# Attention windows: transposes issued later, statistics spread out, depthwise taps moved to earlier stages

## The chip, the cores and the metric

The kernel runs on one core of a Trainium2 chip. Its engines are TensorE (matrix multiplications and transposes, PE in the profile; PEld is its weight load), VectorE (DVE), ScalarE (ACT), GpSimd (POOL) and SyncE (SP), which here only issues DMAs. Each engine works through its own queue in order. The metric is the device time of the whole program in microseconds, as the median of several executions. All times here are microseconds (us) unless marked otherwise.

## The reference

The program is a stack of four layers on `x`, a batch of 4 images with 256 channels of 64 x 64. Each layer is `x = x + layer(_gn(x))`. Layers 0 and 1 are attention layers of one form, with different weights; layers 2 and 3 are Mamba layers, whose code the change leaves alone. Cut to what matters:

```python
def mhsa(x, ...):                       # a gated scan along the height
    Z = tanh(conv1x1(tanh(conv1x1(x, w1a, b1a)), w2a, b2a))
    F = sigmoid(conv1x1(tanh(conv1x1(x, w1b, b1b)), w2b, b2b))
    # second half of the channels is flipped; then, from the last row to the first:
    h = f * h + (1.0 - f) * z

def ssa(x_img, ...):                    # attention of windows
    xw = to_windows(x_img)              # 8 x 8 windows of 8 x 8 pixels
    q, k, v = split(xw @ qkv_w.T + qkv_b)
    logit = einsum('bpc,bqc->bpq', q.mean(2) * SCALE, k.mean(2))
    _, idx = top_k(logit, 4)            # each window attends to 4 windows
    k_g, v_g = gather(k, idx), gather(v, idx)      # 4 * 64 keys
    attn = softmax(einsum('bphqd,bphkd->bphqk', qh * SCALE, kh))   # 8 heads of 32
    out = einsum('bphqk,bphkd->bphqd', attn, vh)
    out_img = from_windows(out) + depthwise_conv3x3(v_img, lepe_w) + lepe_b
    return out_img @ wo_w.T + wo_b

x = x + ssa(mhsa(_gn(x), ...), ...)     # layers 0 and 1
x = x + mamba(_gn(x), ...)              # layer 2
x = x + grouped_mamba(_gn(x), ...)      # layer 3
```

`_gn` normalises groups of two neighbouring image columns, each over all channels and rows: it subtracts the mean and divides by the root of the variance. A strip of the kernel, below, holds four such groups.

## The kernel before

One image is worked on at a time; `x` (256 channels in two halves of 128 partitions, 4096 pixels) stays on the chip through all four layers. The image is cut into 8 strips of 8 columns; a strip holds 8 windows.

**Order of work.** The attention layers run under a manual schedule: the order in which the program issues instructions is the order in which each engine executes them, and tiles are handed on by semaphores as soon as their last reader is done. A tile with `bufs=n` has n buffers; a new tile with the same tag waits until the buffer that it takes is free.

**Scan phase** (`scan_phase`). For each strip s it makes the four small convolutions of the gated scan, the scan on VectorE, and then `keys_values(s - 1)`: keys and values by `conv` (L232), values written into the padded image `vimg` (L357), copied on POOL into `vst` (L361), transposed on TensorE (L383), copied by VectorE and ScalarE into `vn` (L389, L390) and stored with the keys into DRAM. `lepe(lay, s, ...)` gives the steps of the 3 x 3 depthwise convolution of strip s in place in `vimg`, in two halves of the channels, m = 0 and 1: on VectorE nine steps for each m (L268 first, then L270), on POOL 17 for each m (L268 first, then eight pairs of a multiply L253, into a tile of tag "sq" with one buffer, and an add L256). Strips 0 to 4 are done in the scan phase on VectorE. The last call is `keys_values(7)`. Then `routing` finds the four windows for each window (L443 to L464), and the queries of strips 2 to 4 are made, with the m = 0 taps of strip 5 on VectorE between them and the m = 1 taps of strip 5 on POOL.

**Window phase** (`window_phase`). It runs over 32 pairs of windows, i = 0 to 31; `sj, a = divmod(i, 4)` gives the strip and the place in it. The eight heads are worked on in two parities h = 0 and 1. The names of the steps, with their lines:

- `gather(i)` issues eight DMAs on SP (L516) that fetch the keys and values of the pair; the buffers hold four pairs. `indices` loads the window numbers into SP's registers, `double(s)` copies queries (L308, L314).
- `scores(i, h)` on TensorE (L538) into one of two `sc` tiles; `smallest(i, h)` on VectorE (L550) gives the minimum, which is the maximum of the scores since the queries are negated; `exps(i, h, ...)` on ScalarE (L561) has four parts with their sums; `normalise(i, h)` takes the reciprocal on VectorE (L573) and multiplies on POOL in four parts (L576).
- `turn(i, h)` transposes the probabilities with eight instructions on TensorE (L589) into two tiles `pt_ps`, which have two buffers in all, so one turn fills both; `turned(h, 0)` copies the first to `pts` on VectorE (L600), `turned(h, 1)` the second on ScalarE (L602).
- `values(i)` multiplies with the values (L615), and `own_rows(i)` adds the result into `vimg` on VectorE (L626).
- `project(sj - 1, m)` makes the output convolution of a finished strip in the pairs with a = 1 and 2 (14 in all); its `add` (L636) adds into `x` at the pair's end. `query(...)` makes the late queries of strips 6 and 7 in pairs 19, 20, 23 and 24.

In pair i TensorE is given scores(i, 1), turn(i - 1, 1), the projection or query if there is one, scores(i + 1, 0), values(i - 1), turn(i, 0).

**Steps planned into the pairs.** `mids[i]` and `ends[i]` hold steps that run in pair i after the third and fourth exponential of parity 0, and at the pair's end. In the first layer they hold the normalisation of the first two strips for the next layer (`gn`): a sum on VectorE (L143), a column sum on TensorE (L134), the centring on POOL (L151), one square on ScalarE (L156, into a tile of tag "sq", which POOL's taps use too), a reduction (L160), a column sum and the scaling on POOL (L168, L172). In the second layer they hold `stats` of strips 0 to 6: a sum (L200), a column sum (L195), the mean (L206), four squares on ScalarE (L215), a column sum and the variance (L221). All column sums, projections and late queries share one PSUM bank (tag "mm"). What falls behind the last pair is returned in `left` and run by `attention_layers` with the projection of the last strip (`tail`). The taps of strip 6 and 7 are in the window phase: 51 steps on POOL, two per pair, and nine on VectorE in pairs 2 to 10 (`taps`, `dve_taps`).

Of the kernel before, what the change touches and what calls it, by code (L numbers as in the profile page):

```python
# [44 lines left out]
class Net:  # L45
# [33 lines left out]
    def attention_layers(self, x, w_drams, v_drams):  # L79
        tc, nc = self.tc, self.nc  # L80
        with ExitStack() as ctx:
# [107 lines left out]
            def stats(s, psum):  # L189
                xs = x.rearrange("p (c h w) -> p c w h", c=2, w=S)[:, :, strip[s], :]  # L190
                box = {}

                def columns(tag, part):
                    box[tag] = psum().tile([P, NT], F32, tag="mm", name=f"gn_{tag}")
                    nc.tensor.matmul(box[tag][:, 0:4], self.one_gn, part, start=True, stop=True)  # L195

                def sums():
                    box["s1"] = self.small.tile([P, 4], F32, tag="gn_s1", name="gn_s1")
                    xr = x.rearrange("p (n w) -> p n w", w=S)[:, :, strip[s]]
                    nc.vector.tensor_reduce(  # L200
                        box["s1"], xr.rearrange("p n (g t) -> p g n t", t=2), AX.XY, ALU.add
                    )
# [7 lines left out]
                def squares():  # L210
                    box["s2"] = self.small.tile([P, 4], F32, tag="gn_s2", name="gn_s2")
                    sq = norm.tile([P, 2, 8, S], F32, tag="xn", name="gn_sq")
                    for g in range(4):
                        two = slice(2 * g, 2 * g + 2)
                        nc.scalar.activation(  # L215
                            sq[:, :, two], xs[:, :, two], AF.Square,
                            bias=box["mean"][:, g : g + 1], accum_out=box["s2"][:, g : g + 1],
                        )
# [4 lines left out]
                return (  # L223
                    sums, lambda: columns("pm", box["s1"]), mean, squares,
                    lambda: columns("pv", box["s2"]), variance,
                )
# [90 lines left out]
            def scan_phase(lay, work, psum, tail):  # L317
# [78 lines left out]
                for s in range(NW):  # L396
# [32 lines left out]
                    if s in (5, 6):  # L429
                        for evict in [query(lay, s - 5, m, psum) for m in range(2)]:  # L430
                            evict()
                keys_values(NW - 1)

# [35 lines left out]
            def window_phase(lay, work, psum, idx, nxt):  # L469
# [183 lines left out]
                taps6, taps7 = (lepe(lay, s, pool=True) for s in (NW - 2, NW - 1))  # L653
                taps = taps6[17:] + taps7[17:] + taps7[:17]
                dve_taps = lepe(lay, NW - 2)[:9]
# [10 lines left out]
                if nxt:  # L666
                    load_scan_weights(nxt)
                    for s in range(2):
                        i = 10 + s
                        plan(gn(nxt, s, lambda: psum), (ends, i), (ends, i + 1), (mids, i + 2),  # L670
                             (ends, i + 2), (mids, i + 3), (ends, i + 5), (mids, i + 6))
                else:

                    for s in range(NW - 1):
                        i = 4 * s + 6
                        last = i + 6 if s < 5 else i + 3
                        plan(stats(s, lambda: psum), (ends, i), (ends, i + 1), (mids, i + 2),
                             (ends, i + 2), (ends, last), (mids, last + 1))
                for i in range(n_pair):
# [16 lines left out]
                    for t in taps[2 * i : 2 * i + 1]:  # L696
                        t()
# [6 lines left out]
                    exps(i, 1, (0, 1))  # L704
                    scores(i + 1, 0)
# [4 lines left out]
                    turn(i, 0)  # L710
# [21 lines left out]
                turned(0, 0)  # L732
                turned(0, 1)
                turn(n_pair - 1, 1)
                turned(1, 0)
                turned(1, 1)
# [20 lines left out]
            for i, lay in enumerate(layers):  # L757
                with tc.tile_pool(name=f"at_a{i}", bufs=1, reuse_waits="tile") as work, tc.tile_pool(
# [5 lines left out]
                    taps = lepe(lay, NW - 3, psum)[:9]  # L764
# [6 lines left out]
                    for t in lepe(lay, NW - 3, pool=True)[17:]:  # L771
                        t()
                with tc.tile_pool(name=f"at_c{i}", bufs=1, reuse_waits="tile") as work, tc.tile_pool(
# [3 lines left out]
                    box, tail, left = window_phase(lay, work, psum, idx, nxt)  # L777
# [1386 lines left out]
```

## Time and profile before

Three runs took 11993.68, 12002.51 and 12006.19 us, the median 12002.51.

| what | us |
|---|---|
| median of three runs | 12002.51 |
| profiled execution, its own time | 11985.03 |
| its span, first to last instruction | 11983.3 |
| PE busy in the span | 10083.2 (84%) |
| DVE busy | 9833.8 (82%) |
| POOL busy | 8811.5 (74%) |
| ACT busy | 7002.3 (58%) |
| mean granted TensorE clock | 0.932 |

The page lists groups of instructions by line, engine, operation and tiles, with their count, busy time and mean duration in ns, and what ended the engine's idle time before them. A wait reads "engine tile line <- who released it: total us, times, longest". A line of a timeline reads "start, duration, engine, line, operation, tiles, shapes, count [idle before it <- releaser]". The clock is the share of TensorE's full clock that it was granted.

The scan phase and routing of an attention layer take some 215 us, its window phase some 250 us; an image takes about 2995 us, of which the two attention layers are about 950. The window phases begin, by their first minimum reduction, at 233.3, 699.9, 3220.8, 3686.2, 6214.7, 6682.6, 9214.6 and 9678.1 us; first and second layer alternate.

### The profile page before, as it was taken

The numbers are of one execution on the slowest core, as the hardware profiler recorded it, in microseconds if no ns is written. First come the engines' busy times: TensorE is split into PE (matmuls) and PEld (weight loads), VectorE is DVE, ScalarE is ACT, GpSimd is POOL, SyncE is SP. The second block draws the span as 40 slices with busy tenths as digits, with TensorE's granted clock in tenths as the row PEclk, the third lists the DMA queues.
The fourth block names the chain that finished last, engine by engine and source line by source line (L and its number), as shares of the span: only waits on it lengthen the run. The fifth ranks groups of instructions, "written<-read, shape, count | busy, mean of one in ns | idle before, by whom it ended". The sixth has DMA issues, their size and how long they took to land.

```text
span 11983.3 us, 192241 instructions
## 1 busy us (share of the span) xinstructions
PE 10083.2 (84%) x71104; PEld 5778.2 (48%) x71104; DVE 9833.8 (82%) x8350; ACT 7002.3 (58%) x13096; POOL 8811.5 (74%) x6054
## 2 busy tenths in 40 slices
PE   8998887777899888777799988877778998887777
PEld 4564554444455455444445645544444554554444
DVE  6677998998666799899866779989986667998998
ACT  4555555776455555477645555547764555554776
POOL 4666886898456688689745668868984666887897
PEclk9999998999999899899999989989999999998999
DMA  3343454454334355445433434444543343454454
GB/s 96 100 126 134 174 175 149 169 180 160 92 98 127 134 173 177 145 169 182 159 90 99 128 132 173 174 148 167 180 160 91 100 127 135 173 176 146 169 176 154
DMA packets 682506, 1742.10 MB, mean 145 GB/s; under 512 B 88896, under 2 KB 194896, under 8 KB 681312
## 3 DMA queue, kind: packets, MB, share of 16 engines
q1 hardware_dynamic: 676448, 1721.41, 43.1%
q10 hardware_dynamic: 5120, 8.39, 0.3%
q8 instruction: 563, 9.22, 0.3%
q14 instruction: 375, 3.07, 0.1%
HBM read 1601.52 MB, written 94.39 MB: 142 GB/s over the span
## 4 chain that ended last, share of the span: by engine, by line
DVE 23%; PE 23%; ACT 8%; issue 5%; POOL 4%; DMA 1%; SPq 0%; DVEq 0%; POOLq 0%; ACTq 0%
DVE h L1002 13%; DVE pb L996 5%; PE conv_ps L232 4%; PE y L954 4%; PE u_ps L1291 3%; ACT da L938 2%; PE pb L926 1%; PE u_ps L1664 1%; POOL pr L576 1%; PE sc L538 1%; DVE lp L270 1%; PE pt_ps L589 1%; ACT dap L938 1%; PE z_ps L1316 1%; POOL hc L1008 1%
## 5 line engine op out<-in xcount | busy, mean ns | idle before, releaser
L1008 POOL TENSOR_TENSOR hc<-h,cb 128x1024 f32<-128x1024 f32 x2056 | 4809.6, 2350 | 806.4 <-DVE h L1002 350.9
L1002 DVE TENSOR_TENSOR_SCAN h<-da,m_state,pb 128x1024 f32<-128x1024 f32 x1248 | 2920.6, 2340 | 161.4 <-DVE pb L996 2.4
L954 PE MATMUL y<-ident,hc 128*128 128x128 f32 x16384 | 2333.6, 290 | 408.0 <-POOL hc L1008 340.9
L954 PEld LDWEIGHTS y<-ident,hc 128*128 128x128 f32 x16384 | 2034.5, 150 | 1124.9 <-POOL hc L1008 577.0
L996 DVE TENSOR_TENSOR pb<-du,pb 128x1024 f32<-128x1024 f32 x1672 | 2025.4, 1211 | 113.4 <-PE pb L926 110.9
L938 ACT ACTIVATE da<-delta,m_v 128x1024 f32<-128x1024 f32 x1672 | 1899.5, 1141 | 135.5 <-DVE h L1002 118.3
L926 PE MATMUL pb<-m_parts,pick 128*128 128x512 bf16 x3312 | 1078.2, 410 | 846.1 <-DVE h L1002 777.6
L576 POOL TENSOR_SCALAR pr<-pr,sm,zero 128x256 f32<-128x256 f32 x2048 | 1136.5, 569 | 476.8 <-DVE sm L573 475.8
L561 ACT ACTIVATE pr<-sc,mn 128x256 f32<-128x256 f32 x2048 | 955.9, 482 | 647.5 <-DVE sm L573 480.9
L926 PEld LDWEIGHTS <-pick 128*128 128x128 bf16 x3312 | 263.1, 101 | 1787.4 <-DVE h L1002 981.2
L550 DVE TENSOR_REDUCE mn<-sc 128x4 f32<-128x1024 f32 x512 | 627.9, 1228 | 550.0 <-PE sc L538 547.2
L1002 DVE TENSOR_TENSOR_SCAN h<-da,pb 128x1024 f32<-128x1024 f32 x424 | 969.5, 2287 | 55.1 <-DVE pb L996 0.9
L912 POOL TENSOR_TENSOR bb<-du,bb 128x1024 f32<-128x1024 f32 x376 | 888.6, 2363 | 88.8 <-DMA bb<-m_cd 84.0
L589 PE MATMUL pt_ps<-ident,pr 128*128 128x128 f32 x4096 | 705.4, 304 | 144.3 <-POOL pr L576 51.1
L1002 DVE TENSOR_TENSOR_SCAN h<-dap,m_state,bb 128x1024 f32<-128x1024 f32 x288 | 672.4, 2335 | 65.1 <-ACT dap L938 45.9
L232 PE MATMUL conv_ps<-att_y,att_wb 128*128 128x512 f32 x1536 | 683.3, 594 | 1.3 <-DVE gn_mean L206 1.3
L589 PEld LDWEIGHTS pt_ps<-ident,pr 128*128 128x128 f32 x4096 | 490.3, 151 | 307.5 <-POOL pr L576 161.7
L538 PE MATMUL sc<-kv,q_swap 32*64 32x128 f32 x8192 | 597.2, 287 | 6.7 <-DMA kv<-kv_dram 4.7
L938 ACT ACTIVATE dap<-delta,m_v 128x1024 f32<-128x1024 f32 x376 | 419.7, 1116 | 304.0 <-DVE h L1002 234.2
L538 PE MATMUL sc<-kv,att_y 32*64 32x128 f32 x7168 | 569.2, 287 | 11.8 <-DMA kv<-kv_dram 7.5
L538 PEld LDWEIGHTS sc<-kv,att_y 32*64 32x64 f32 x7168 | 430.0, 139 | 144.9 <-ACT pr L561 65.6
L270 DVE SCALAR_TENSOR_TENSOR lp<-vimg,att_v,lp 128x512 f32<-128x512 f32 x616 | 465.4, 756 | 28.1 <-DVE lp L270 1.4
(300 smaller groups left out, 17937.9 us busy)
## 6 DMA issues: line engine op xcount, KB each, us to landing
cb<-m_cd SPq DMA_DIRECT2D x2048, 512.0 KB, 3.8
kv<-kv_dram SPq DMA_DIRECT2D x1984, 128.0 KB, 2.8
bb<-m_cd SPq DMA_DIRECT2D x376, 512.0 KB, 5.4
kv_dram<-kst SPq DMA_DIRECT2D x128, 256.0 KB
kv_dram<-vn SPq DMA_DIRECT2D x128, 256.0 KB, 4.1
q_swap<-att_y SPq DMA_DIRECT2D x96, 256.0 KB, 4.3
m_pe<-in_pe_dram SPq DMA_DIRECT2D x32, 512.0 KB, 4.1
out_dram<-yo SPq DMA_DIRECT2D x64, 256.0 KB, 2.4
```

What stands on the lines that cost most here:

```text
L232: nc.tensor.matmul(ps, w[:, k, w0 + m * P : w0 + (m + 1) * P], src[:, k], start=(k == 0), stop=(k == 1),)
L538: nc.tensor.matmul(sc[h][b * 64 : b * 64 + 64, r, w, m, :], (own(sj, m) if r == b else swap[sj % 2][:, m])[rows, 2 * a + w], kv[i, w][rows ...
L561: nc.scalar.activation(t[:, g].rearrange("p j r t -> p r j t"), sc[h][:, :, g // 2, g % 2, :].rearrange("p r (j t) -> p r j t", j=2), AF.E ...
L576: nc.gpsimd.tensor_scalar(t[:, g], t[:, g], s[:, g : g + 1], self.zero, ALU.mult, ALU.add)
L589: nc.tensor.transpose(pt[h][j][:, g, :], t[:, g, j].rearrange("p r t -> p (r t)"), self.ident,)
L912: nc.gpsimd.tensor_tensor(pb[i], slots[i][0]["du"], pb[i], ALU.mult)
L926: nc.tensor.matmul(pb[i][:, ss], self.pick[:, n : n + 1].to_broadcast([P, P]), blk["parts"][:, ss], start=True, stop=True,)
L938: nc.scalar.activation(da[i], blk["delta"], AF.Exp, scale=blk["a"](n))
L954: nc.tensor.matmul(blk["y"][:, ss], t[:, ss], self.ident, is_transpose=True, start=(n == 0 and ss.start % NT == 0), stop=(n == DS - 1 and ...
L996: nc.vector.tensor_tensor(pb[i], blk["du"], pb[i], ALU.mult)
L1002: nc.vector.tensor_tensor_scan(h[i][:, ss], da[i][:, ss], pb[i][:, ss], state, ALU.mult, ALU.add)
L1008: nc.gpsimd.tensor_tensor(hc[i][:, ss], h[i][:, ss], cb[i][:, ss], ALU.mult)
```

## The change

- **Turns.** turn(i, 0) is no longer issued within pair i but at the start of pair i + 1, ahead of scores(i + 1, 1). turn(i - 1, 1) is issued in pair i ahead of scores(i + 1, 0), behind the steps of `mids` and the projection or query, where it was directly behind scores(i, 1). The evictions `turned` keep their places.
- **Squares, sums and norms.** In `stats` the four squares become four steps, each at a place of its own (end of one pair, middle and end of the next, middle of the third). The sum moves one pair later (a = 3, where there is no add); column sums follow in pairs with a = 0 and a = 3. In `gn` the two strips begin at pairs 7 and 11 and not at 10 and 11, and the square stands one pair behind the centring. The statistics of strip 6 fall behind the last pair.
- **Taps.** The m = 0 taps of strip 5 (nine, VectorE) and its m = 1 taps (17, POOL) go to the end of the scan phase: the nine and the first five of POOL ahead of keys_values(7), the other twelve behind it. The m = 0 taps of strip 6 take the place of those of strip 5 between the queries, nine of its POOL steps stand behind these, and the other eight go into the window phase. Strip 7 has its m = 1 taps on POOL in the window phase and its m = 0 taps on VectorE there. So POOL has 25 steps in the window phase, one per pair, and VectorE nine, in pairs with a = 0 or 3 from i = 3 to 19.

```diff
+                def square(g):
+                    if g == 0:
+                        box["s2"] = ...
+                        box["sq"] = norm.tile([P, 2, 8, S], F32, tag="xn", name="gn_sq")
+                    two = slice(2 * g, 2 * g + 2)
+                    nc.scalar.activation(
+                        box["sq"][:, :, two], xs[:, :, two], AF.Square,
+                        bias=box["mean"][:, g : g + 1], accum_out=box["s2"][:, g : g + 1],
+                    )
...
+                for t in lepe(lay, NW - 3, psum)[:9]:
+                    t()
+                later = lepe(lay, NW - 3, pool=True)[17:]
+                for t in later[:5]:
+                    t()
                 keys_values(NW - 1)
+                for t in later[5:]:
+                    t()
...
-                taps6, taps7 = (lepe(lay, s, pool=True) for s in (NW - 2, NW - 1))
-                taps = taps6[17:] + taps7[17:] + taps7[:17]
-                dve_taps = lepe(lay, NW - 2)[:9]
+                taps = taps + lepe(lay, NW - 1, pool=True)[17:]
+                dve_taps = lepe(lay, NW - 1)[:9]
...
-                        i = 10 + s
+                        i = 7 + 4 * s
                         plan(gn(nxt, s, lambda: psum), (ends, i), (ends, i + 1), (mids, i + 2),
-                             (ends, i + 2), (mids, i + 3), (ends, i + 5), (mids, i + 6))
+                             (ends, i + 3), (mids, i + 4), (ends, i + 4), (mids, i + 5))
...
-                        i = 4 * s + 6
-                        last = i + 6 if s < 5 else i + 3
+                        i = 4 * s + 7
                         plan(stats(s, lambda: psum), (ends, i), (ends, i + 1), (mids, i + 2),
-                             (ends, i + 2), (ends, last), (mids, last + 1))
+                             (ends, i + 2), (mids, i + 3), (ends, i + 3), (mids, i + 4),
+                             (ends, i + 4), (mids, i + 5))
...
                     if i:
+                        turn(i - 1, 0)
                         scores(i, 1)
                         turned(0, 0)
                         turned(0, 1)
-                        turn(i - 1, 1)
                         smallest(i, 1)
...
                     normalise(i, 0)
-                    for t in taps[2 * i : 2 * i + 1]:
-                        t()
...
                     exps(i, 1, (0, 1))
+                    if i:
+                        turn(i - 1, 1)
                     scores(i + 1, 0)
                     if i:
                         turned(1, 0)
                         turned(1, 1)
                         values(i - 1)
-                    turn(i, 0)
...
-                    for t in taps[2 * i + 1 : 2 * i + 2]:
+                    for t in taps[i : i + 1]:
                         t()
-                    for t in dve_taps[i - 2 : i - 1] if i > 1 else ():
-                        t()
+                    if a in (0, 3) and i and dve_taps:
+                        dve_taps.pop(0)()
...
-                    taps = lepe(lay, NW - 3, psum)[:9]
+                    taps = lepe(lay, NW - 2, psum)[:9]
...
-                    for t in lepe(lay, NW - 3, pool=True)[17:]:
+                    later = lepe(lay, NW - 2, pool=True)[17:]
+                    for t in later[:9]:
                         t()
...
-                        for t in (left[0], tail[0], left[1], tail[1], g[0], left[2], left[3], *g[1:]):
+                        var, left = left[0], left[1:]
+                        for t in (var, tail[0], left[0], left[1], tail[1], *left[2:6], g[0],
+                                  left[6], left[7], *g[1:]):
                             t()
```

More of the change, by code (lines that the diff above doesn't have):

```diff
@@ L208, in mean @@
                     )
[L210 to L218, printed above, removed]
+                def square(g):
+                    if g == 0:
+                        box["s2"] = self.small.tile([P, 4], F32, tag="gn_s2", name="gn_s2")
+                        box["sq"] = norm.tile([P, 2, 8, S], F32, tag="xn", name="gn_sq")
[4 more added lines that the diff above has]
+                    )
                 def variance():
@@ L223, in stats @@
                 return (
-                    sums, lambda: columns("pm", box["s1"]), mean, squares,
+                    sums, lambda: columns("pm", box["s1"]), mean,
+                    *(lambda g=g: square(g) for g in range(4)),
                     lambda: columns("pv", box["s2"]), variance,
@@ L465, in routing, with window_phase @@
                 return idx
-            def window_phase(lay, work, psum, idx, nxt):
+            def window_phase(lay, work, psum, idx, nxt, taps):
                 vec, wb = lay["vec"], lay["wb"]
@@ L731, in window_phase @@
                         t()
[L732 to L736, printed above, removed]
+                for h in range(2):
+                    turn(n_pair - 1, h)
+                    for j in range(2):
+                        turned(h, j)
                 values(n_pair - 1)
@@ L776, in attention_layers @@
                     nxt = layers[i + 1] if i + 1 < len(layers) else None
-                    box, tail, left = window_phase(lay, work, psum, idx, nxt)
+                    box, tail, left = window_phase(lay, work, psum, idx, nxt, later[9:])
                     if nxt is None:
```

## The prediction

> **What bounds the kernel now.** I read the chain of work on the page first: VectorE and TensorE each carry 23% of it, and its largest lines (L1002, L996, L954) belong to the Mamba layers, which the change does not touch. What it touches is the window phase, which runs eight times (two attention layers, four images). So next came the stretches from the first to the last minimum reduction (L550) of each window phase; here are the two of the third image (columns: length, busy time of PE, PEld, DVE, ACT, POOL with counts, granted clock, DMA share, GB/s):
>
> ```profile
> 6214.70:6467.70 253.00, 230.28 (x4503) 167.72 (x4494) 160.92 (x250) 155.96 (x571) 197.08 (x305) 0.89 0.49 146
> 6682.60:6935.60 253.00, 233.75 (x4520) 174.28 (x4512) 165.58 (x260) 170.80 (x617) 185.66 (x300) 0.89 0.47 142
> ...
> sum 2009.10, PE 1822.86 PEld 1331.07 DVE 1308.32 ACT 1305.21 POOL 1530.78; mean PE 227.86 PEld 166.38 DVE 163.54 ACT 163.15 POOL 191.35
> ```
>
> All eight take 248 to 253 us, 2009 us of 11983; TensorE is the fullest engine and runs at a granted clock of 0.89 to 0.93. How near to its work is it? Pairs 20 to 23 of the first layer (6388.2 to 6417.1) take 28.9 us with TensorE busy for 28.28 at clock 1.00: a pair with a 256-channel projection or query in it takes 7.2 us and has no air. A pair without one takes 6.0 us (pair 4: 6249.08 to 6255.06 between its L550 starts). Pairs 1 to 30 hold 18 of the first kind and 12 of the second: 18 x 7.2 + 12 x 6.0 = 202 us, against 241 measured in either layer. About **39 us per window phase** are stalls and slow clock; that is all the change can touch. The list of waits of TensorE, second layer, third image, says what they are:
>
> ```profile
> PE pt_ps L589 <- DVE pts L600: 6.8, 7, 1.3
> PE pt_ps L589 <- ACT pts L602: 3.2, 5, 1.2
> PE pt_ps L589 <- POOL pr L576: 3.0, 13, 0.6
> ```
>
> The transposes of a parity wait until the evictions of the parity before have freed the two transpose banks. One such place in the timelines of VectorE and TensorE:
>
> ```profile
> 6736.95 0.97 DVE L270 SCALAR_TENSOR_TENSOR vimg<-vimg,att_v 128x512 f32<-128x512 f32 x1
> 6737.84 1.35 DVE L636 SCALAR_TENSOR_TENSOR x<-conv_ps,att_v,x 128x512 f32<-128x512 f32 x1
> 6739.22 1.22 DVE L200 TENSOR_REDUCE gn_s<-x 128x4 f32<-128x1024 f32 x1
> 6740.36 0.68 DVE L600 COPY pts<-pt_ps 128x512 f32<-128x512 f32 x1
> ...
> 6741.10 0.66 PE L589 MATMUL pt_ps<-ident,pr 128*128 128x128 f32 x4 [1.29 <-DVE pts L600]
> ```
>
> A tap (0.97), the residual add (1.35) and the statistics sum (1.22) stand ahead of the copy; TensorE waits for it. Straight after, the clock falls:
>
> ```profile
> 6738.00:6742.20 4.20, 2.56 (x44) 1.60 (x40) 4.17 (x6) 1.15 (x5) 2.17 (x4) 1.00 0.65 193
> 6742.20:6755.90 13.70, 13.70 (x238) 11.78 (x230) 7.66 (x15) 9.83 (x34) 10.99 (x17) 0.50 0.29 91
> ```
>
> TensorE worked 2.56 of 4.20 us, then had half the clock for 13.7 us. The two pairs there take 8.7 and 8.0 us, not 6.0: 4.7 us lost, **0.34 us for each us at half clock**.
>
> **The change, part by part.**
>
> *Turns.* turn(i,0) moves past the SP work at a pair's end (8 gathers, the doubling, the index loads), the steps in `ends` and the first two exponentials of ScalarE. On TensorE nothing but a statistics column stands between the old place and the new, and SP's gathers wait for values(i-1), not for the turn: zero, at worst a 0.3 us column before it. turn(i-1,1) moves from ahead of the projection, query or column to behind it. Where there is none (12 pairs) the order of every engine stays. In the 18 others it starts 1.72 us later (four matmuls of 0.43), so evictions and POOL's normalising have that much more time. Today it takes about 1.43 us there instead of 1.07, paced by POOL: up to 0.35 x 14 projections = 4.9 us per window. Queued behind the later turn is turned(1,1) on ScalarE and behind that the last two exponentials: mn(i,1) allows them 3.9 us after the scores begin, the new turn about 4.4; the scores that need their bank start at 6.9. Covered by 1.5 us.
>
> *Squares, second layer.* Four L215 squares in a row hold ScalarE for 3.0 us (6753.24 to 6756.23) and with it the exponentials and the copy L602. One at a time (0.73 us) they fit: ScalarE has some 1.7 us idle before a pair's first exponentials and 0.7 to 1.0 before its third.
>
> *Sums, second layer.* The sum leaves the pair with an add for the next one. There it may share VectorE with a tap (0.97 + 1.22, pairs 7, 11, 15, 19), without an add. A tap and sum there would put the copy about 0.8 us past its use in pairs 8, 12 and 16; pair 20 has a query as cover. I charge 3 x 0.8 = 2.4 us in the second layer, 2 x 0.8 = 1.6 in the first.
>
> So for the **second layer**: of the 10.0 us of waits for L600 and L602 I count three quarters, 7.5; from the paced transposes 2.0 (they overlap those waits, bounds 0 and 4.9); minus 2.4. The clock: 0.89 over 253 us is 55.7 us at half, 19 us lost. It drops where TensorE stalls; I let four tenths of it go, 7.6 (bounds 0 and 13). Sum 14.7 us.
>
> [...]
>
> *Norms, first layer.* Waits of ScalarE, third image:
>
> ```profile
> ACT gn_sq L156 <- POOL vimg L256: 12.9, 2, 6.6
> ```
>
> The square (L156) and POOL's taps share one buffer ("sq"); ScalarE waits with all exponentials behind it until the tap's add has ended. That stays: strips 0 and 1 are squared after pairs 10 and 14, which again end in such an add. The wait is shorter, as the centring (2.47 us) now ran a pair earlier: from the last exponential, reciprocal at +1.7, normalising 2.16, add 1.19 = 5.2 us, not 6.3 to 6.6. Scaling (1.64 + 1.90 on POOL) still stands ahead of a normalise. Pairs 11 to 17 take 68.0 us (6305.27 to 6373.32) against 45.6 free of stalls, 22.4 over; afterwards I make it 2 x 4.6 (square) + 2 x 1.9 (scale) + 2 x 0.5 (centre) + 7 (clock) = 21. Gain 1.5.
>
> *Taps.* POOL drops from two steps per pair to one (0.77 or 1.19 us); it is not the fullest engine, so the value is in the paced transposes, counted. VectorE's nine taps leave pairs 2 to 10 for pairs without an add. **First layer** together: 4.9 (turns) + 1.5 + a quarter of the 19 us of clock, 4.7 - 1.6 = 9.5 us (bounds -5 and 22).
>
> *Taps moved ahead.* At the end of the scan phase, ahead of keys_values(7), come nine VectorE taps (7.2 us by the same nine at 6141.52) and five POOL steps (4.9 us by 6195.94 to 6200.85):
>
> ```profile
> 6198.44 0.69 DVE L389 COPY vn<-vt_ps 128x512 f32<-128x512 f32 x1 [7.10 <-PE vt_ps L383]
> ...
> 6193.62 0.67 POOL L361 COPY vst<-vimg 128x512 f32<-128x512 f32 x1 [5.12 <-ACT vimg L357]
> ...
> 6219.79 2.16 POOL L576 TENSOR_SCALAR pr<-pr,sm,zero 128x256 f32<-128x256 f32 x4 [6.13 <-DVE sm L573]
> ```
>
> They fit into 7.10 and 5.12 us idle: 0.1 us late, with the store of V behind it. POOL's 21 steps after routing (17 now) take 4.3 us more, in an idle time of 6.13 here and 4.92 at least in the eight phases. Without this cover they would cost 7.2, 4.9 and 4.3.
>
> *Tail.* Strip 6's statistics now fall wholly behind the last pair; column, mean and the last projection share one bank: about 0.9 us, and a sum ahead of a copy 0.4: 1.3 us per image.
>
> **Sum.** (14.7 + 9.5) x 4 = 96.8, less 4 x 1.3 and 8 x 0.1, is 90.8. The profiled execution took 11985.0 us (span 11983.3): 11894.2. The median shown, 12002.5, lies 17.5 above it: **11912 us**.
>
> **Rivals.** (a) *The stalls go and the clock with them*: the second layer's 39 us less 4 lost in pairs 1 to 4, where little changes, and 9 left for columns and shared taps, 26, and half of the first's, 19: 45 x 4 = 180, so 11822. For: stalls feed the clock. Against: the first-layer squares still block. (b) *Hidden anyway*: SP needs about 6.0 us per pair (8 gathers x 0.65 and an index load) and sets the pace wherever TensorE falls below it; or the clock falls regardless of the stalls. If only projection pairs gain, 14 x 8 x 0.2 = 22 us: 11980. Against: SP idles about 1 us per pair where TensorE is full. (c) *Slower: the wait moves to ScalarE.* In 144 pairs with a projection or query, turned(1,1) holds the last exponentials. If turns there end more than 1.5 us later than I make them, because POOL's normalising is late, each further us costs 144 us; 0.63 us over the slack cancels the gain, 1.0 gives 12056. For: POOL's normalise carries 20% of the first layer's chain. Against: it ends before the turn's new start in pairs 20 to 30. (d) *The change doesn't do what it says*: for parity 0 that is so (TensorE's order stays); it is in the sum as zero.
>
> **How the numbers follow.** Mine 0.56 (11850 to 11960), (a) 0.14, (b) 0.16, (c) 0.14. Range 11830 to 12010: beyond it lie the better half of (a) and most of (c). A measurement here tells 0.2%, 24 us, from no change. Faster: mine, (a) and a third of (b), 0.76; same 0.10; slower 0.14.
>
> **What would show it.** Waits of L589 for L600 and L602 in the second layer at 3 us or less; granted clock there 0.93 or more; no run of four L215; pairs 21, 22, 25 of the second layer near 7.2, not 7.9 to 8.5; L156 still waiting for L256, near 5 us each; the idle of 7.10 before L389 gone. Wrong if L561 waits for L602's turn, or the clock stays at 0.89 with the stalls gone.

## The result, and the profile after

The kernel after took 11970.14 us, the median of seven runs (11945.93 to 11990.24), against 11998.07 us for the kernel before beside it (11983.79 to 12006.19): a ratio of 0.9974, with a 95% interval of 0.9962 to 0.9985. That is **28 us faster where 90 were forecast**. The profiled execution of after was the slowest of its seven (11990.24 us, span 11988.5), that of before (11985.03) near the fast end of its own; so the two spans, taken whole, show no gain. The window phases do. Between first and last minimum reduction (now L558), with the columns of the prediction (length, busy PE, PEld, DVE, ACT, POOL with counts, clock, DMA share, GB/s), the eight of after are these:

```profile
232.80:486.50 253.70, 232.05 (x4499) 173.77 (x4491) 161.75 (x250) 157.85 (x570) 176.98 (x284) 0.87 0.51 145
701.90:943.60 241.70, 219.96 (x4517) 164.82 (x4509) 163.87 (x258) 173.21 (x614) 164.84 (x278) 0.94 0.52 148
...
6225.80:6474.80 249.00, 227.24 (x4503) 169.72 (x4494) 162.01 (x249) 157.74 (x571) 176.77 (x283) 0.89 0.52 148
6690.80:6934.80 244.00, 221.36 (x4518) 163.28 (x4509) 163.39 (x258) 172.98 (x614) 164.88 (x278) 0.93 0.51 146
...
sum 1981.10, PE 1801.48 PEld 1343.26 DVE 1303.46 ACT 1323.03 POOL 1365.88; mean PE 225.19 PEld 167.91 DVE 162.93 ACT 165.38 POOL 170.74
```

The sum fell from 2009.10 to 1981.10, by 28.0 us. The first layer's phases stand at a mean of 250.9 us (250.1 before), the second layer's at 244.4 (252.1): 4 x 7.7 us won in the second layer, and no gain in the first. The forecast was 4 x 14.7 and 4 x 9.5. That the phases give the same 28 us as the medians is in part luck: a second profile of the kernel before (the run e11 below) has a sum of 1995.0. The time outside the phases is not read as the change's: it was 9974.3 us in the first profile of before and 10002.1 in the second, with the same program; in the kernel after it was 10007.

What TensorE waits for in the second layer of the third image:

```profile
PE conv_ps L233 <- DVE gn_mean L206: 8.5, 6, 1.4
PE sc L546 <- DMA kv<-kv_dram: 4.5, 4, 2.5
PE conv_ps L233 <- DVE gvar L221: 3.4, 2, 2.0
PE ov_ps L623 <- ACT pts L610: 2.8, 5, 0.8
PE pt_ps L597 <- POOL pr L584: 1.5, 6, 0.6
```

The 10.0 us of waits of the transposes for the evictions (L600 and L602, now L608 and L610) are gone, as forecast, and the transposes paced by POOL fell from 3.0 to 1.5. In their place stands something that the prediction never named: **the projection and the late query (L233) wait 11.9 us**, in eight places, for the mean (L206) and the variance (L221). VectorE and TensorE at two of them:

```profile
6844.27 1.21 DVE L200 TENSOR_REDUCE gn_s<-x 128x4 f32<-128x1024 f32 x1
6845.40 0.68 DVE L608 COPY pts<-pt_ps 128x512 f32<-128x512 f32 x1
6845.99 1.21 DVE L558 TENSOR_REDUCE mn<-sc 128x4 f32<-128x1024 f32 x1
6847.13 0.14 DVE L221 COPY gvar<-gn_pv 128x4 f32<-128x4 f32 x1
...
6856.31 1.22 DVE L558 TENSOR_REDUCE mn<-sc 128x4 f32<-128x1024 f32 x1 [0.81 <-PE sc L546]
6857.45 0.15 DVE L206 TENSOR_SCALAR gn_mean<-gn_pm 128x4 f32<-128x4 f32 x1
```

```profile
6845.06 0.27 PE L546 MATMUL sc<-kv,att_y 32*64 32x128 f32 x1
6847.33 3.46 PE L233 MATMUL conv_ps<-att_y,att_wb 128*128 128x512 f32 x4 [2.00 <-DVE gvar L221]
...
6853.89 0.39 PE L195 MATMUL gn_pm<-gn_s,one_gn 128*128 128x4 f32 x2 [0.17 <-ACT att_y L299]
6854.14 1.07 PE L597 MATMUL pt_ps<-ident,pr 128*128 128x128 f32 x8
...
6855.97 0.27 PE L546 MATMUL sc<-kv,att_y 32*64 32x128 f32 x1
6857.65 1.56 PE L233 MATMUL conv_ps<-vimg,att_wb 128*128 128x512 f32 x3 [1.42 <-DVE gn_mean L206]
```

The column sum (L195) fills the one bank of tag "mm". The step that empties it stands in `mids`, on VectorE behind the minimum reduction mn(i, 1), and that one waits for the scores. The matmuls of L233 need the same bank. From the end of the scores to the next matmul TensorE has nothing: a reduction of 1.22 us and the mean, 1.42 us in all. The kernel before had the same queue on VectorE, and turn(i-1, 1) on TensorE in just that gap; there, in the same pair (20) of the same image:

```profile
6843.43 1.23 DVE L550 TENSOR_REDUCE mn<-sc 128x4 f32<-128x1024 f32 x1 [0.93 <-PE sc L538]
6844.57 0.15 DVE L206 TENSOR_SCALAR gn_mean<-gn_pm 128x4 f32<-128x4 f32 x1
...
6842.04 0.28 PE L195 MATMUL gn_pm<-gn_s,one_gn 128*128 128x4 f32 x2
6843.29 1.33 PE L589 MATMUL pt_ps<-ident,pr 128*128 128x128 f32 x8
6844.78 1.98 PE L232 MATMUL conv_ps<-att_y,att_wb 128*128 128x512 f32 x4 [0.16 <-DVE gn_mean L206]
```

The turn that moved was the cover of the column's way through VectorE; the runs e2 and e4 below test that. And this stall is paid a second time: in the 3.4 us up to 6846.91 TensorE was busy for 54%, and from 6846.91 to 6850.33 its clock was halved, so the four matmuls behind the wait of 2.00 us take 3.46 us and not 1.98.

In the first layer the square's wait is there, shorter, as forecast (12.9 before):

```profile
ACT gn_sq L156 <- POOL vimg L257: 8.5, 2, 4.3
```

### The profile page after: what moved, and what is told of

Same layout as the page of the kernel before. It is cut to its first block, busy times and chain, and to the rows that moved or that the text cites. A ratio compares the mean times of both kernels' runs of the same rounds, so it can differ in the third digit from the quotient of the medians.

```text
span 11988.5 us, 192249 instructions
## 1 busy us (share of the span) xinstructions
PE 10125.6 (84%) x71104; PEld 5815.7 (49%) x71104; DVE 9886.2 (82%) x8422; ACT 7025.3 (59%) x13096; POOL 8695.8 (73%) x5918
## 5 line engine op out<-in xcount | busy, mean ns | idle before, releaser
L558 DVE TENSOR_REDUCE mn<-sc 128x4 f32<-128x1024 f32 x512 | 629.5, 1231 | 345.4 <-PE sc L546 344.5
L233 PE MATMUL conv_ps<-att_y,att_wb 128*128 128x512 f32 x1536 | 696.9, 604 | 13.6 <-DVE gvar L221 13.6
L597 PE MATMUL pt_ps<-ident,pr 128*128 128x128 f32 x4096 | 630.8, 296 | 62.0 <-ACT pts L610 27.4
L608 DVE COPY pts<-pt_ps 128x512 f32<-128x512 f32 x512 | 355.2, 694 | 280.0 <-PE pt_ps L597 279.4
L271 DVE SCALAR_TENSOR_TENSOR lp<-vimg,att_v,lp 128x512 f32<-128x512 f32 x672 | 507.7, 755 | 30.8 <-DVE lp L271 1.0
```

The costliest lines, as they stand in the source:

```text
L233: nc.tensor.matmul(ps, w[:, k, w0 + m * P : w0 + (m + 1) * P], src[:, k], start=(k == 0), stop=(k == 1),)
L597: nc.tensor.transpose(pt[h][j][:, g, :], t[:, g, j].rearrange("p r t -> p (r t)"), self.ident,)
```

## The experiments

Two yardsticks: the ratio to the kernel before, run beside it on the same chip, and, from each profile, the mean length of the four window phases of either layer. "Half clock" is the time in them at a granted clock of 0.5, summed from the clock's records.

| kernel | ratio, 95% interval | first layer, us (half clock) | second layer, us (half clock) |
|---|---|---|---|
| before | 1 | 250.1 (42.7) | 252.1 (44.4) |
| before again (e11) | one run | 248.4 (41.8) | 250.4 (42.7) |
| after | 0.9974, 0.9962 to 0.9985 | 250.9 (58.0) | 244.4 (36.7) |
| e1 after, turns back | 0.9925, 0.9908 to 0.9941 | 247.2 (44.4) | 229.0 (17.1) |
| e2 before, turns moved | 1.0050, 1.0033 to 1.0067 | 248.2 (52.9) | 263.1 (65.7) |
| e3 before, statistics and norms moved | 0.9924, 0.9908 to 0.9941 | 250.2 (45.2) | 227.3 (11.1) |
| e4 after, mean and variance read early | 0.9925, 0.9908 to 0.9941 | 249.5 (59.7) | 228.5 (27.3) |
| e5 after, taps with a tile of their own | 0.9935, 0.9918 to 0.9951 | 240.6 (39.3) | 241.4 (31.6) |
| e6 e3, sum again behind the add | 0.9983, 0.9976 to 0.9990 | 252.1 (52.9) | 240.8 (29.0) |
| e7 e3, four squares again in a row | 0.9933, 0.9916 to 0.9949 | 248.7 (46.9) | 229.8 (8.5) |
| e8 e1, e4 and e5 together | 0.9881, 0.9864 to 0.9897 | 237.3 (25.6) | 228.2 (17.9) |
| e9 before, turn of parity 0 moved | 1.0025, 1.0013 to 1.0036 | 252.8 (47.8) | 255.7 (54.6) |
| e10 after with e4 and e5 | 0.9875, 0.9858 to 0.9891 | 235.4 (28.2) | 232.2 (35.0) |

The two profiles of the kernel before differ by 1.7 us in either layer's mean; differences of that size are not read. Among the 104 window phases of these 13 profiles, phases of one kernel and layer differ by 0.25 us for each us at half clock (a fitted line, standard error 0.02). The prediction read 0.34 from a single stretch.

**The turns, undone and alone.** e1 is the kernel after with the turns at their old places, and e2 is the kernel before with nothing but the turns moved. The edit of e1, against after (e2 is its reverse, against before):

```diff
                     if i:
-                        turn(i - 1, 0)
                         scores(i, 1)
                         turned(0, 0)
                         turned(0, 1)
+                        turn(i - 1, 1)
...
                     exps(i, 1, (0, 1))
-                    if i:
-                        turn(i - 1, 1)
                     scores(i + 1, 0)
...
                         values(i - 1)
+                    turn(i, 0)
```

> The changed kernel with both turns at their old places; statistics, norms and taps as changed. Theory A (bank): behind the scores the projection now waits for the mean or variance to leave the one mm bank, 11.9 us per second-layer window phase and 2.8 per first; the turn, put back ahead of the projection, covers 1.07 of each wait. So the waits of the projection for gn_mean and gvar fall under 4 us in the second layer, the waits of the turns for the evictions come back with 2 to 5 us, and the second-layer window phase (first to last minimum reduction, 244.4 us on average in the changed kernel) is 240 to 246, the whole within 30 us of the changed kernel. Theory B (something else sets the pace, SP or the clock): the bank waits vanish as well, but the window phase stays within 2 us. Forecast's view, that the turns alone bring 4.9 us per window phase: the whole 20 to 40 us slower than the changed kernel.

> The kernel before with the turns moved and nothing else. Theory A: the variance still sits in the bank at a = 1, so the projection waits 1.4 us there in seven pairs of the second layer, 10 us, against 4 to 7 us of eviction waits saved: second layer 250 to 256 us (252.2 before), first layer 246 to 250 (250.1 before, no statistics in most pairs), the whole between 10 us faster and 20 slower than before. Theory B: the same. Forecast's view: 4.9 us per window phase, 40 us faster.

e1 took 11906.23 us, e2 12047.14, the kernel before beside them 11991.14. So the turns alone **cost 56 us** (0.50%), and taking them out of the kernel after wins 0.49%. The two measurements, from opposite sides, agree. Both lie outside what I had expected: under theory A, e1 was to stay within 30 us of the kernel after, and e2 to end between 10 us faster and 20 slower than before. In the second layer the turns cost 11.0 us a phase alone and 15.4 in the kernel after. The waits of TensorE in e2, second layer of the third image, put the new stall where no statistics step had been touched:

```profile
PE conv_ps L232 <- DVE gvar L221: 8.5, 6, 1.4
PE pt_ps L589 <- DVE pts L600: 4.2, 4, 1.3
...
PE conv_ps L232 <- DVE gn_mean L206: 2.8, 2, 1.4
```

**The statistics alone.** e3 is the kernel before with the new `stats`, `gn` and the steps behind the last pair, without turns and taps.

```diff
-                        i = 4 * s + 6
-                        last = i + 6 if s < 5 else i + 3
+                        i = 4 * s + 7
                         plan(stats(s, lambda: psum), (ends, i), (ends, i + 1), (mids, i + 2),
-                             (ends, i + 2), (ends, last), (mids, last + 1))
+                             (ends, i + 2), (mids, i + 3), (ends, i + 3), (mids, i + 4),
+                             (ends, i + 4), (mids, i + 5))
```

> The kernel before with the squares, sums and norms spread and nothing else (turns and taps at their old places). Theory A: the second layer keeps the turn as cover of the bank wait, loses the bursts of squares and the sum behind the add: 240 to 246 us (252.2 before); the first layer is unchanged or up to 8 us slower, as its two squares now block ScalarE in two separate places: 250 to 258 (250.1 before). The whole 0 to 50 us faster. Theory B: second layer not under 248. Forecast's view: second layer 244, first layer 249.

It took 11902.2 us: 89 us faster than the kernel before, three times what the whole change gives. The second layer fell by 24.8 us a phase, below the 240 to 246 us of theory A and the 244 of the forecast's view; the first layer didn't move. e1, which is e3 with the taps moved as well, differs from it by 4 us, within their intervals: the moved taps bring and cost nothing that can be seen. In e3's second layer, third image, these are all the waits of TensorE that the list gives:

```profile
PE pt_ps L590 <- POOL pr L577: 4.3, 19, 0.6
PE ov_ps L616 <- ACT pts L603: 4.0, 8, 0.9
PE sc L539 <- DMA kv<-kv_dram: 0.6, 2, 0.3
PE conv_ps L233 <- DVE gn_mean L206: 0.5, 3, 0.2
PE conv_ps L233 <- DVE gvar L221: 0.4, 2, 0.2
```

**Which part of the statistics.** e6 puts the sum back into the pair with the add; e7 puts the four squares back in a row, at the end of a pair with a = 1 (in the kernel before, a = 0). Both start from e3. The edit of e6, then that of e7:

```diff
-                        plan(stats(s, lambda: psum), (ends, i), (ends, i + 1), (mids, i + 2),
+                        plan(stats(s, lambda: psum), (ends, i - 1), (ends, i + 1), (mids, i + 2),
```

```diff
-                             (ends, i + 2), (mids, i + 3), (ends, i + 3), (mids, i + 4),
+                             (ends, i + 2), (ends, i + 2), (ends, i + 2), (ends, i + 2),
```

> The kernel of the statistics alone, with the sum put back behind the add (one pair earlier, a = 2); squares, columns and norms stay spread. It takes the sum's share out of the gain of 24.8 us that the statistics alone brought in the second-layer window phase (252.1 to 227.3). If the sum behind the add is the larger cause, the phase is 238 to 246 us and the waits of the turns for VectorE's copies come back with 4 to 6 us; if the squares are, it is 229 to 234. The forecast counted both alike: 236 to 240.

> The kernel of the statistics alone, with the four squares in a row at the end of a pair (a = 1) and the rest spread. If the row of squares is the larger cause of the 24.8 us, the second-layer window phase is 238 to 246 us, with waits of the turns for ScalarE's copies of 3 us or more; if the sum is, 229 to 234. The forecast counted both alike: 236 to 240.

With the sum back the second layer's phase is 13.5 us longer than e3's, and one line is back on TensorE's list:

```profile
PE pt_ps L590 <- DVE pts L601: 6.0, 6, 1.3
```

With the squares in a row it is 2.5 us longer, little more than two profiles of one kernel differ by. So putting the sum back costs 13.5 of the 24.8 us, putting the squares in a row some 2.5. If the parts add up, which no run tests, the other 9 belong to what both leave in place: the second column and the variance at new pairs, and the statistics of strip 6 behind the last pair. Pair 29 alone, by the mean of the four phases, takes 7.8 us in e3, and 11.1 and 10.0 in the two profiles of before. I didn't part these any further.

**Is it the bank?** e4 is the kernel after, turns moved as they are, with the mean and the variance read ahead of the evictions and of mn(i, 1), so that the bank comes free while TensorE still works on the scores.

```diff
-                mids, ends, left = {}, {}, []
+                starts, mids, ends, left = {}, {}, {}, []
...
-                        plan(gn(nxt, s, lambda: psum), (ends, i), (ends, i + 1), (mids, i + 2),
+                        plan(gn(nxt, s, lambda: psum), (ends, i), (ends, i + 1), (starts, i + 2),
...
-                        plan(stats(s, lambda: psum), (ends, i), (ends, i + 1), (mids, i + 2),
+                        plan(stats(s, lambda: psum), (ends, i), (ends, i + 1), (starts, i + 2),
                              (ends, i + 2), (mids, i + 3), (ends, i + 3), (mids, i + 4),
-                             (ends, i + 4), (mids, i + 5))
+                             (ends, i + 4), (starts, i + 5))
...
                         scores(i, 1)
+                        for t in starts.get(i, ()):
+                            t()
                         turned(0, 0)
```

> The changed kernel with the mean and the variance read out of the mm bank at the start of a pair, ahead of the first eviction on VectorE, and not behind the minimum reduction; nothing else. This takes away what the projection waits for. Theory A: waits of the projection for gn_mean and gvar (11.9 us per second-layer window phase, 2.8 per first) under 2 us; the second layer 228 to 236 us, not 244.4, the first 247 to 251, not 250.9; the whole 35 to 75 us faster than the changed kernel. Theory B: the waits go but the time reappears as waits for gathered keys or at half clock; second layer 240 or more, the whole within 20 us of the changed kernel.

It took 11907.18 us: all that the turns had cost is back, with the turns still moved. The second layer's phase is 15.9 us shorter than in the kernel after: 11.6 us of waits are gone, and the 9.4 us less at half clock are worth some 2 to 3 us, an estimate from the 0.25 and 0.34 above. TensorE's list in the second layer of the third image (the waits of L233 come to 0.3 us, from 11.9):

```profile
PE sc L546 <- DMA kv<-kv_dram: 2.2, 6, 0.5
PE pt_ps L597 <- POOL pr L584: 1.9, 6, 0.6
...
PE conv_ps L233 <- DVE gvar L221: 0.3, 1, 0.3
```

The pairs show the same. Mean of the four second-layer phases, us from one minimum reduction of parity 1 to that of the next pair:

| pair | 20 | 21 | 22 | 23 | 24 | 25 |
|---|---|---|---|---|---|---|
| before | 7.6 | 7.9 | 8.5 | 6.8 | 7.6 | 7.9 |
| after | 10.0 | 9.1 | 6.9 | 7.1 | 9.7 | 9.5 |
| e4 | 7.0 | 7.2 | 6.9 | 7.3 | 7.4 | 7.2 |

Pair 22, where no mean or variance stands between scores and projection, wins in both. Pairs 20, 21, 24 and 25 lose 7.3 us together in the kernel after and win 2.2 with the bank free early.

**Turn of parity 0 alone.** e9 is the kernel before with turn(i - 1, 0) ahead of scores(i, 1). Moved only to just ahead of the steps in `ends`, the turn leaves the order of every engine's instructions as it was; so all that e9 changes is that the column of `ends` comes ahead of the turn.

```diff
                     if i:
+                        turn(i - 1, 0)
                         scores(i, 1)
...
                         values(i - 1)
-                    turn(i, 0)
```

> The kernel before with only the turn of parity 0 moved to the start of the next pair. On TensorE only a statistics column changes sides with it. Theory A: nothing, 252.1 +- 3 us in the second layer and 250.1 +- 3 in the first, the whole within 24 us of before; all of the 50 us that the two turns lost together (second layer 263.1) then belongs to parity 1. Rival: the columns, which wait for an add or an eviction to free the bank, now hold this turn too, and cost 1 us in each of 14 places of the second layer, half of the loss.

It took 12038.61 us against 12004.07 beside it: **34 us slower** for a swap that I had booked at zero. The second layer's phases are 3.6 us longer than in the first profile of before (two of the four carry that: 259.4 and 260.2 us), the first layer's 2.7. The waits of L232 for mean and variance are hardly longer (0.9 us a phase; 0.7 before in the phase listed in the prediction). One place is seen: at the end of pair 29 the second column waits for the add (L636) to free the bank, and the turn, which stood ahead of it, now stands behind. Second layer, third image, before and then e9:

```profile
PE gn_pv L195 <- DVE x L636: 1.0, 1, 1.0
...
PE gn_pv L195 <- DVE x L636: 2.0, 1, 2.0
```

That is 1.0 us in each of four phases, 4 of the 34. The time at half clock is longer too, by 10.2 us a phase in the second layer and 5.1 in the first: at 0.25 to 0.34 us each some 15 to 21 us, an estimate. Why a column of 0.3 us moves the clock so far isn't settled. In the kernel after, whose columns stand in other pairs, the turn of parity 0 wasn't moved alone; with the bank read early (e4) the total shows no loss by it.

**The square and the taps.** e5 is the kernel after with a tile of its own for the taps, so that the square needn't wait for a tap's add.

```diff
-                        both = norm.tile([P, 2, 8, S], F32, tag="sq", name="tap", bufs=1)
-                        box[m] = both[:, m]
+                        box[m] = norm.tile([P, 8, S], F32, tag="tap", name="tap", bufs=1)
```

> The changed kernel with a buffer of their own (tag tap) for the weighted taps on POOL, so that the square of the norms no longer waits for a tap's add; nothing else. Theory C (the norms of the first layer are bound by that shared buffer): the wait of ScalarE for POOL ahead of the square (8.5 us per first-layer window phase) falls under 1, pairs 11, 12, 15 and 16 lose 3 to 5 us each, the first layer is 234 to 242 us, not 250.9; the whole 30 to 65 us faster than the changed kernel, the second layer unchanged at 244 +- 3. Rival C' (the centring and scaling on POOL, ahead of a normalise, set these pairs, the square is only one of several): first layer 246 or more, the whole within 20 us.

It took 11916.18 us: 0.39% of the time, 47 us, below the kernel after by the two ratios. The first layer fell by 10.3 us a phase; pairs 11 and 15, where the square stands, from 12.4 and 12.8 us to 7.8 and 6.6. Pairs 12 and 16 stay at 11.0 and 10.6. There POOL scales the strip ahead of the normalising of both parities, which pile up behind it to 4.83 us in one run; e5's timeline of POOL:

```profile
6288.82 1.65 POOL L168 TENSOR_TENSOR gn_rstd<-gn_rstd,minus_half 128x8 f32<-128x8 f32 x1 [2.74 <-DVE sm L580]
6290.54 1.90 POOL L172 TENSOR_TENSOR att_xn<-att_xn,gn_rstd 128x1024 f32<-128x1024 f32 x1
6292.42 4.83 POOL L583 TENSOR_SCALAR pr<-pr,sm,zero 128x256 f32<-128x256 f32 x8
```

**Put together.** e8 has the turns at their old places, the early reading and the taps' own tile; e10 has the last two and the turns moved.

> The changed kernel with the turns at their old places, the mean and variance read out of the bank at the start of a pair, and a buffer of their own for the taps. Theory A and C together: second layer 225 to 230 us (229.0 with the turns back alone), first layer 232 to 242 (247.2 with the turns back alone); the whole 25 to 60 us under the kernel with the turns back (11906), so 11845 to 11880. If C is wrong the first layer stays at 245 or more and the whole at 11895 to 11915.

> The changed kernel with its turns as it has them, the mean and variance read out of the bank at the start of a pair, and a buffer of their own for the taps: the partner of the kernel that has the turns back (11849). It asks what the moved turns bring once nothing holds the bank. Theory A: the forecast's 4.9 us per window phase were pacing by POOL that is gone anyway when its taps are halved: window phases within 3 us of the partner's 237.3 and 228.2, the whole 11830 to 11870. Forecast's view: 30 to 40 us faster than the partner, 11810 to 11820.

e8 took 11849.2 us (11841.58 to 11858.59), 1.19% below the kernel before: **faster than both kernels**. Its eight window phases come to 1861.60 us:

```profile
6153.70:6387.90 234.20, 218.37 (x4502) 158.90 (x4491) 159.62 (x250) 156.44 (x571) 176.17 (x283) 0.96 0.55 157
6603.60:6832.90 229.30, 215.37 (x4517) 159.11 (x4507) 161.76 (x258) 170.75 (x614) 164.81 (x277) 0.96 0.54 156
...
sum 1861.60, PE 1739.53 PEld 1278.17 DVE 1285.78 ACT 1307.04 POOL 1364.91; mean PE 217.44 PEld 159.77 DVE 160.72 ACT 163.38 POOL 170.61
```

e10 is its equal (11858.3, with intervals that overlap). With the bank out of the way, a moved turn does shorten a pair with a projection, from 7.2 to some 7.0 us (pairs 22 and 26 of the second layer 6.9 to 7.0 against 7.2), but the phases spend more time at half clock (35.0 us against 17.9 in the second layer) and the gain is not kept.

**Before again.** e11 is the kernel before under the profile a second time, as a measure of how far two profiles of one program stand apart.

> The kernel before, profiled once more, to see how much of the time outside the window phases moves with the execution: 9974 us in the first profile of before, 10007 in that of the changed kernel, with the same code in the Mamba layers. If it is the clock's phase, this one lies between 9974 and 10010 and the window phases again at 250.1 and 252.1 +- 2; if the change lengthened the Mamba layers, it is 9974 +- 5.

11998.9 us; window phases 1.7 us shorter on average than in the first profile, the rest of the span 27.8 us longer. Hence the rule used above: compare the phases, not the spans. The phases move too, by 14 us in the sum of eight.

## Why the prediction was right and wrong

Sign and range held; the size did not. The forecast was 90 us, the measurement 28. Parted by the runs:

| part | forecast, us | measured, us |
|---|---|---|
| turns (4.9 and 2.0 per phase, times 4) | -28 | +56 to +59 (e2; after against e1) |
| squares, sums, norms, taps, tail (the other 63) | -63 | -85 (e1), -89 (e3, without the taps) |
| together | -91 | -28 |

- **Turns: the step that failed.** The prediction booked a gain of 28 us for starting the turn of parity 1 later, and asked only what is queued behind it at its new place (turned(1, 1) and the last exponentials), with 1.5 us of slack. For TensorE the slack held. ScalarE's copy does wait longer for the turn (second layer, third image, before and after), but there no scores wait for the exponentials behind it:

```profile
ACT pts L602 <- PE pt_ps L589: 11.9, 10, 2.8
...
ACT pts L610 <- PE pt_ps L597: 34.7, 31, 3.7
```

The prediction didn't ask what the turn had been standing in front of. It had covered the way of mean and variance from the bank through VectorE, 1.07 us of work in a gap of 1.4 to 2.0. That mean, variance, projections and queries share one bank was known, and yet the move of this turn behind the column was charged with nothing; 0.3 us at worst was allowed for the other turn. Instead of the gain there were 11.9 us of waits of L233 a second-layer phase. e4 takes these away, leaves the turns moved, and has the time of e1 (11907 and 11906 us): the loss in the kernel after hangs on them. In the first layer the pacing by POOL, for which 4.9 us were booked, did ease: with the turns alone (e2) those waits fell from 9.0 to 5.0 us a phase, the mean of four. But 4.4 us of new waits of L232 for mean and deviation (L149, L167) stand against it, and no gain can be read (248.2 us against 250.1 and 248.4).
- **Turn of parity 0 as zero: wrong** by 34 us in the kernel before (e9), with a mechanism that is mostly not seen. Rival (d) falls with it. As e2 holds both turns and lost 56, the one of parity 1 leaves some 22 of that, if the two add up; it wasn't run alone.
- **Rival (c), the slower one,** had the right sign for the turns and the wrong place: the wait moved to TensorE's L233, not to ScalarE.
- **Sums and squares: right, and under-sized.** I counted 7.5 us of stalls, 7.6 of clock and a charge of 2.4 for a tap and a sum in one pair: 12.7 without the turns' 2.0. e3 measured 24.8. Time at half clock fell by 33.3 us, at 0.34 some 11.3 against 7.6, at 0.25 some 8.3. The rest, 13.5 to 16.5, stands against 7.5 less 2.4 and is the term most out. Of the waits for L600 and L602 not three quarters but all went, 9.2 us in the phase itself (the 10.0 of the prediction has 0.8 from behind its end), and no wait shows for the 2.4 charged; what makes up the remainder wasn't parted. The squares in a row (e7) were worth some 2.5.
- **Norms: wrong.** Pairs 11 to 17 of the first layer take 74.1 us in the kernel after, where the forecast has 45.6 and 21, that is 66.6. The waits for L257 came out a little below the 5.2 forecast, 4.3. But the pairs with a square still take 12.4 and 12.8 us, and the quarter of the clock's loss that I let go did not go: 58.0 us at half clock against 42.7 (45.2 in e3, without moved turns and taps). Without moved turns the new places of square and scale bring nothing that can be seen (e3, 250.2). What was left to win there is the shared tile, 10.3 us a phase (e5).
- **Taps moved ahead: right.** The copy of V's transpose (now L390) comes at 6210.58 straight behind the taps, its 7.10 us of idle time filled; POOL's first normalise of the window idled 0.94 us where it had 6.13. The four scan segments took 215.6, 217.1, 214.9 and 215.4 us before and 215.4, 215.8, 216.0 and 215.0 after.
- **Tail: right in kind.** From the last minimum reduction to the next step behind the phase, an image takes 0.8 us more on average; the forecast was 1.3. The second profile of before lies 0.4 above the first.
- **The signs named in advance.** Waits for L600 and L602 under 3 us: none left. No run of four squares: none (the first two stand at 6767.36 and 6770.58). Clock 0.93 in the second layer: 0.94, 0.91, 0.93, 0.92. Pairs 21, 22 and 25 near 7.2 us: 6.9 for 22, but 9.1 and 9.5 for 21 and 25; these two were the sign of the failed step.

## What to carry to other kernels

Before moving work on an in-order engine, list what stood behind it and was waiting for something else: work that is ready early may be the cover of another engine's round trip (here 1.07 us of turn in a gap of 1.4 to 2.0). Where small statistics share an accumulation bank with large matmuls, place the read that frees the bank ahead of any instruction that waits for the same engine; here that gave back 59 us. And when a change of several parts gains a little, run the parts alone: here one part won 89 us and another lost 56.

## What the runs showed of the hardware

**The clock fell behind stretches in which TensorE was partly idle.** The prediction had one row for this; all eight window phases of the kernel before can now be counted. In them the half-clock stretches came in multiples of 3.413 us (28 of 53 are 3.4 us long, the longest 20.5), so I laid a grid of 3.413 us on the clock's records. In front of 53 drops the window had TensorE busy for 58 to 65% (the middle half; 28% at least, 85% at most); in the 434 windows that kept the full clock it was 96% in the median, 78% or more in all but one in twenty, and 63% at the least. Of 46 windows less than two thirds busy, 40 were followed by a drop. The longest idle stretch in the 3.4 us ahead of a drop was 2.47 us, on average 1.16. So here **a drop mostly followed a window less than two thirds busy**, and none followed a wholly idle one; 13 drops came behind fuller windows. This is a count and no experiment: what sets the clock isn't shown by it. Leaving the transposes out of the count parts the two kinds of windows worse: 50 windows ahead of a drop and 114 that kept the clock then lie under one half. The same count in the kernel after and in e3 gives 46 and 26 drops.

One thing was seen and not tried: in the second layer the scores wait 3.3 to 4.8 us a phase on average for the gathered rows (kv) in the kernel after and in e1, e4, e8 and e10 (2.1 in e5), and 1.5 at most in those without the moved taps (before, e2, e3, e6, e7, e9). In the third image of the kernel after 2.5 us of it stand at one place, pair 7. Whether it is the taps' doing, or the gathers set the pace once TensorE is fuller (rival (b)), no run tells; the total of e1 against e3 shows no loss by it.
